# The second cross-attention layer's scores, softmax and attention rewritten in the form of the first layer's

## The chip, the cores and the metric

The kernel runs on one core of a Trainium2 chip. The time is device microseconds of one execution. The kernel before took 649.7 us, the median of three runs (649.56 to 650.06).

A core has TensorE (PE, matmuls; an fp32 matmul shows as two records in the profile), VectorE (DVE), ScalarE (ACT), GpSimd (POOL) and SyncE (SP, which here issues most of the loads). Each engine works through its own queue in order. Matmuls write to PSUM, in tiles of 128 × 512 fp32, of which the program has eight; everything else lies in SBUF.

## The reference

Two cross-attention layers over eight batches: 100 queries of 1024 features, 1444 context rows of 512 features. All is fp32.

```python
# layer 0
Q = query @ Wq + bq;  K = key @ Wk + bk;  V = key @ Wv + bv
weights = softmax(Q @ K.T / sqrt(1024), axis=-1)      # over the 1444 context rows
x = query + (weights @ V) @ Wo + bo
# layer 1
q = x @ Wq + bq;  k = latent @ Wk + bk;  v = latent @ Wv + bv
w = softmax(q @ k.T / sqrt(1024), axis=1)             # over the 100 queries
y = w @ v + x
out = (y - mean(y)) * rsqrt(var(y) + 1e-6) * gamma + beta
```

The axes of the two softmaxes differ: the first layer normalises over the context rows, the second over the queries of one batch. So in the second layer the weights of a context row sum to one, and those of a query don't: their sum, a column of 100 numbers per batch, multiplies `bv`.

## The kernel before

*Algebra.* The weight matrices are multiplied together first (Wq·Wk and, in layer 0, Wv·Wo), in the seven products of a Strassen-Winograd scheme (`weight_products`, `seven_products`). Then `queries(layer, …)` turns the queries into `gT[layer]`, 512 features by 400 queries per half of the batches, and scores are products of these with the raw context. Attention multiplies weights with the raw context, and the value projection comes after it (`project0`, and in layer 1 `project1_halves` for batches 0 to 4, `project1` for 5 and 6, `project_last` for 7). In these projections VectorE adds each product onto the residual `xT` (L585, L755), and some later products add onto the PSUM banks of earlier ones. Bias terms of the keys come in as one number per query (`c0`, `c1`).

*Layer 0.* The context comes in twice: as features (`load_features`, 128 features by 1444 rows, four loads `cT` per batch) and as rows (`load_rows`, chunks of 120 rows by 512 features, four units `c`). Scores (`scores0`, L528) have the queries loaded as weights and the features streamed, so they come out 100 queries by 1444 rows; in four PSUM banks. ACT copies them to `prob` with scale and bias (L541), VectorE takes maxima, ACT exponentials and normalises, and VectorE transposes the result in blocks of 32 × 32 to rows by queries (`transposed`, L563, 16 instructions of 12 blocks each per 32 partitions). Where that would be late, a few chunks are transposed by TensorE (`first_transposed`, L578). Attention (`weighted_rows`, L496) has the context rows loaded as weights and streams the 100 weights columns; it yields 512 features by 100 queries.

*Layer 1.* Scores (`scores1`, L643) have context columns loaded and stream the queries, so they come out 120 rows by 100 queries, and the softmax over queries is along the free axis. A PSUM bank holds a group of four chunks; for each of three groups VectorE scales and adds the bias (L653), takes maxima (L661), ACT does four exponentials with sums (L663), and VectorE reciprocal and product (L666, L667). Attention of batches 0 to 5 (`attend1`, L703) has the weights loaded and streams the context rows with a column of ones behind them (the memsets L470), so that the last column gives the sum of a query's weights; four TensorE transposes (`attended`, L723) turn it round. For batches 6 and 7 it is `weighted_rows`, and the sums come from VectorE (`weight_sums`, L679 to L681) and a transpose (`weight_totals`, L687).

*Order.* TensorE's order is written out by hand: the scores, attention and finishing routines are generators that yield after each matmul, and the loops at the end interleave them. A stage is the attention of batch b (48 matmuls) beside the scores of batch b+2 (44 steps in layer 0, 48 in layer 1). The first two batches' scores stand alone before the stages; in layer 0 the scores of the last batch run two steps to one. After stage 5 of layer 1 `project1_halves` runs with no attention beside it; batches 6 and 7 have `finish` routines (transposes L774, layer norm L778 to L797, output) beside their attention. The other engines' queues are put in order by a scheduler when the program is built.

*Memory.* One pool `stream` of ten equal units holds context loads and, earlier, weights. `weight_rows` has three buffers, `prob` three (in layer 1 these hold `bv`, `gamma` and `beta`, one number per feature, repeated on all partitions by `row_on_all`, L867). PSUM: six banks in `bank`, two in `bank2`.

## Time and profile before

| what | value |
|---|---|
| median of three runs | 649.7 us |
| the profiled execution | 649.66 us, of which 647.9 us from first to last instruction |
| granted TensorE clock, mean | 0.996 |
| bytes moved | 127.49 MB, 197 GB/s mean |
| layer 0: two batches' scores | 190.2 to 210.1 us |
| layer 0: stages and attention of the last batches | 210.1 to 350.3 us |
| projection and layer 1's queries | 350.3 to 426.2 us |
| layer 1: two batches' scores | 426.2 to 447.9 us |
| layer 1: six stages | 447.9 to 569.2 us |
| half-projection (`project1_halves`) | 569.2 to 593.0 us |
| last two batches, finishing | 593.0 to 647.9 us |

The profile page gives, for each engine, the busy time, its share of the span and the number of instructions; below it the span in 40 equal slices of 16.2 us with the busy tenths of each. A group line names the line of the program, the engine, the operation, output and inputs, and the shapes. The timeline gives the start, the length and the group; successive matmuls overlap a little, so the time of one is taken from start to start. In the second layer's stages the other engines' busy time is:

```profile
core 0: us, PE busy (x) PEld busy (x) DVE busy (x) ACT busy (x) POOL busy (x), PEclk, DMA share, GB/s
...
488.00:508.00 20.00, 20.00 (x196) 20.00 (x195) 5.69 (x12) 5.78 (x28) 0.41 (x4) 1.00 0.92 299
```

### The profile page before, as it was taken

To read this page: it belongs to the slowest core of one execution; us is meant where nothing else is said; L and a number is where in the kernel's file an instruction comes from. 1 tells how busy PE (TensorE), PEld (TensorE's weight loads), DVE (VectorE), ACT (ScalarE), POOL (GpSimd) and SP (SyncE) were. 2 spreads that over 40 slices of the span, in tenths; PEclk is the share of its full clock that TensorE was granted. 3 is DMA by queue.
4 is the path that set the end of the run, shared out by engine and by line. 5 is a ranking of instruction groups with operands and counts; after the bars stand their busy time and mean duration, and the time that the engine had idled before them with its cause. 6 is when DMAs were issued, how large, how long until landed. Compare 5 with 4: busy or idle time off the path is not lost.

```text
span 647.9 us, 10121 instructions
## 1 busy us (share of the span) xinstructions
PE 637.1 (98%) x4120; PEld 530.4 (82%) x4120; DVE 395.9 (61%) x751; ACT 122.6 (19%) x325; POOL 64.0 (10%) x81
## 2 busy tenths in 40 slices
PE   9999999999999999999999999999999999999994
PEld 7886445568885999999998555589999999989992
DVE  5999949569624775566753784266322223566984
ACT  1010010101104223322320001113222322210221
POOL 5000000019100000000000000000000000000673
PEclk9999999999999999999999999999999999999998
DMA  8928028000099888898998002038889999920212
GB/s 297 385 100 299 0 75 309 0 1 0 2 342 335 272 305 310 314 313 313 336 352 300 1 12 119 0 115 265 284 314 290 314 305 292 309 84 1 65 64 76
DMA packets 60234, 127.49 MB, mean 197 GB/s; under 512 B 3928, under 2 KB 22972, under 8 KB 60188
## 3 DMA queue, kind: packets, MB, share of 16 engines
q1 hardware_dynamic: 57742, 119.92, 54.2%
q0 software_dynamic: 2048, 6.56, 3.1%
q8 instruction: 32, 0.52, 0.3%
q10 hardware_dynamic: 398, 0.36, 0.2%
q14 instruction: 14, 0.11, 0.1%
HBM read 123.56 MB, written 3.28 MB: 196 GB/s over the span
## 4 chain that ended last, share of the span: by engine, by line
PE 81%; issue 11%; POOL 4%; DMA 1%; DVE 1%; POOLq 0%; ACT 0%; SPq 0%
PE A L496 12%; PE s L528 12%; PE s L643 10%; PE A L703 6%; PE qk_x L135 5%; PE g_x L135 5%; PE qk_y L135 4%; PE g_y L135 3%; PE vo_x L135 3%; PE o_x L135 3%; POOL z L796 3%; PE qk_w L135 2%; PE vo_y L135 2%; PE A1r L703 2%; PE o_y L135 2%
## 5 line engine op out<-in xcount | busy, mean ns | idle before, releaser
L496 PE MATMUL A<-w,c 120*128 120x100 f32 x960 | 145.0, 267 | 0.0
L496 PEld LDWEIGHTS A<-w,c 120*128 120x128 f32 x960 | 130.1, 191 | 0.3
L643 PE MATMUL s<-g1T,cT 128*120 128x100 f32 (+1 forms) x768 | 123.2, 261 | 0.0
L528 PE MATMUL s<-cT,g0T 128*100 128x131 f32 (+2 forms) x592 | 119.0, 296 | 0.0
L643 PEld LDWEIGHTS s<-g1T,cT 128*120 128x120 f32 (+1 forms) x768 | 105.2, 185 | 0.6 <-issue 0.3
L528 PEld LDWEIGHTS s<-cT,g0T 128*100 128x100 f32 x592 | 77.6, 167 | 8.3
L703 PE MATMUL A<-c,w 120*100 120x128 f32 (+1 forms) x432 | 83.0, 273 | 0.0
L563 DVE STREAM_TRANSPOSE w<-prob 32x384 f32<-32x384 f32 (+1 forms) x128 | 68.6, 536 | 15.3 <-ACT prob L549 12.5
L703 PEld LDWEIGHTS A<-c,w 120*100 120x100 f32 (+1 forms) x432 | 55.5, 168 | 0.0
L663 ACT ACTIVATE w<-w,negmax 120x100 f32<-120x100 f32 (+1 forms) x96 | 35.1, 366 | 76.7 <-DVE negmax L661 76.7
L653 DVE SCALAR_TENSOR_TENSOR w<-s,c 120x400 f32<-120x400 f32 (+1 forms) x24 | 13.8, 574 | 56.5 <-PE s L643 56.5
L541 ACT ACTIVATE prob<-s,c 100x394 f32<-100x394 f32 (+3 forms) x32 | 18.0, 563 | 94.5 <-PE s L528 94.3
L438 POOL TENSOR_SCALAR xT<-xT,L_xattn_bo 128x800 f32<-128x800 f32 x8 | 20.8, 2610 | 133.3 <-PE qk_x L135 133.3
L542 DVE TENSOR_REDUCE maxima<-prob 100x1 f32<-100x394 f32 (+3 forms) x32 | 16.3, 527 | 24.1 <-ACT prob L541 23.8
L135 PE MATMUL qk_x<-qk 128*128 128x256 f32 x128 | 29.1, 383 | 0.4 <-DMA qk<-in_L_xattn_WkT 0.4
L703 PE MATMUL A1r<-c,w 120*100 120x129 f32 x144 | 27.8, 274 | 0.0
L135 PEld LDWEIGHTS qk_x<-qk 128*128 128x128 f32 x128 | 23.8, 191 | 4.9 <-issue 1.4
L666 DVE RECIPROCAL rtotal<-total 120x4 f32<-120x4 f32 (+1 forms) x24 | 4.2, 176 | 28.9 <-ACT w L663 28.9
L277 DVE SCALAR_TENSOR_TENSOR qk_L_xattn_bk<-qk,L_xattn_bk,qk_L_xattn_bk 128x1024 f32<-128x1024 f32 x14 | 17.9, 1277 | 4.3 <-DMA qk<-in_L_xattn_WqT 4.2
L470 POOL MEMSET c<- 128x3 f32 x24 | 2.5, 104 | 162.7 <-PE s L643 140.0
L703 PEld LDWEIGHTS A1r<-c,w 120*100 120x100 f32 x144 | 18.5, 168 | 0.0
L585 DVE TENSOR_TENSOR xT<-xT,o_x 128x400 f32<-128x400 f32 (+1 forms) x24 | 13.7, 601 | 7.9 <-PE o_x L135 7.5
(230 smaller groups left out, 917.9 us busy)
## 6 DMA issues: line engine op xcount, KB each, us to landing
c<-in_ctx SPq DMA_DIRECT2D x48, 768.0 KB, 7.8
cT<-in_ctxT SPq DMA_DIRECT2D x32, 728.0 KB, 7.2
cT<-in_ctxT SPq DMA_DIRECT2D x32, 722.0 KB, 6.6
c<-in_ctx SPq DMA_DIRECT2D x16, 512.0 KB, 8.5
vo<-in_L_xattn_Wo SPq DMA_DIRECT2D x8, 512.0 KB, 6.4
qk<-in_L_xattn_WqT SPq DMA_DIRECT2D x8, 512.0 KB
qk<-in_L_xattn_WqT SPq DMA_DIRECT2D x15, 256.0 KB, 5.3
qk<-in_L_xattn_WkT SPq DMA_DIRECT2D x15, 256.0 KB, 6.7
```

Source lines behind the costliest of these rows:

```text
L135: nc.tensor.matmul(banks[n // per][:, n % per * width : (n % per + 1) * width], lhs[i][:, n * P : (n + 1) * P], rhs[i], start=(fresh and i ...
L277: nc.vector.scalar_tensor_tensor(acc, src, cols[v][:, h : h + 1], acc, ALU.mult, ALU.add)
L438: nc.gpsimd.tensor_scalar(xT[:, e, :], xT[:, e, :], out_bias[:, e : e + 1], None, ALU.add)
L496: nc.tensor.matmul(ps[:, k * T : (k + 1) * T], c[m // CQ][:r, m % CQ, k * P : (k + 1) * P], w[:r, m, :], start=(m == 0 and k == 0), stop=( ...
L528: nc.tensor.matmul(banks[n // per][:T, cuts[n] - o : cuts[n + 1] - o], q0[:, k, t0 : t0 + T], cT[k][:, cuts[n] : cuts[n + 1]], start=(k == ...
L541: nc.scalar.activation(p[:, o:e], ps[:T, : e - o], AF.Identity, bias=c0[:T, b : b + 1], scale=SCALE)
L542: nc.vector.tensor_reduce(parts[:, n : n + 1], p[:, o:e], AX.X, ALU.max)
L563: nc.vector.transpose(blocks(w, r, m0 * T + q * QD, T, MC - m0), blocks(p, q, m0 * MR + r * QD, MR, MC - m0),)
L643: nc.tensor.matmul(ps[:r, (m - m0) * T : (m - m0 + 1) * T], cT[m // CQ][:, k, o : o + r], q1[:, k, t0 : t0 + T], start=(k == 0), stop=(k = ...
L663: nc.scalar.activation(w[:r, m, :], w[:r, m, :], AF.Exp, bias=negmax[:r, m : m + 1], accum_out=total[:r, m : m + 1])
L703: nc.tensor.matmul(to, w[:r, m, :], c[m // CQ][:r, m % CQ, k * P : (L + 1 if k == LC - 1 else (k + 1) * P)], start=(m == 0 and k in (0, LC ...
L796: nc.gpsimd.tensor_tensor(z, z, beta[:T], ALU.add)
```

## The change

The second layer takes the first layer's routines, which become common ones (`scores`, `alternated`, `first_scores`).

- Scores: queries loaded as weights, features streamed (`load_features` in place of `load_columns`); ACT copies the raw scores, scaled and with the bias, to `prob`.
- Key bias: `key_biases`, as in layer 0, one column per batch, for both halves before the first scores; the matmuls against `ones` (L620) go.
- The raw scores are transposed by VectorE (`transposed`, 16 instructions) for batches 1 to 7; for batch 0 by TensorE, in three groups of four chunks placed between the scores of batch 1. Then the softmax by rows as before (`softmax_rows`), without the L653 step.
- Attention is `weighted_rows` for all batches; `attend1`, `attended` and the ones column go.
- The weights' sums: for every batch seven GpSimd instructions (`weight_sums`), and for each pair of batches two TensorE transposes and one VectorE reduction (`weight_totals`), at the ninth step of the odd batch's attention.
- The operand sums of the half-projection (`project1_sums`, eight instructions) move from VectorE to GpSimd.
- `gamma`, `beta` and the two halves of `bv` lie in two units of `stream`, for the whole of layer 1, and come in four GpSimd-issued loads; `prob` is used for scores.
- Layer 1's last scores run two steps to one, too.

Layer 0's work stays as it was.

```diff
     def unit(name):
-        return stream.tile([P, CQ * (L + 1)], F32, tag="unit", name=name)
+        return stream.tile([P, E + L], F32, tag="unit", name=name)
...
-    def left_sums(A, S, some=(0, 1, 2, 3)):
+    def left_sums(A, S, some=(0, 1, 2, 3), engine=nc.vector):
         A11, A12, A21, A22 = A
         todo = ((S[0], A21, A22, ALU.add), (S[1], S[0], A11, ALU.subtract))
         todo += ((S[2], A11, A21, ALU.subtract), (S[3], A12, S[1], ALU.subtract))
         for n in some:
-            combine(*todo[n])
+            combine(*todo[n], engine)
...
+    def key_biases(name, kb, bqbk):
+        sums = quarter_sums(name)[:, :B, :]
+        t = row(f"{name}_t").rearrange("p (b q j) -> p b q j", q=P // QD, j=QD)
+        for g in range(B // G):
+            src = bass.AP(kb[g].tensor, kb[g].offset, [list(kb[g].ap[0]), [T, G], [QD, P // QD], [1, QD]])
+            nc.vector.transpose(t[:, g * G : (g + 1) * G], src)
+        nc.vector.tensor_reduce(sums, t, AX.X, ALU.add)
+        c = totals(name, sums, B)
+        nc.vector.tensor_scalar(c, c, SCALE, bqbk, ALU.mult, ALU.add)
+        return c
...
-    def load_columns(b):
...
-    def load_rows(b, summed=False):
+    def load_rows(b):
         src = a["ctx_512"][b]
         for q in range(NQ):
             t = unit(f"c_{b}_{q}").rearrange("p (c l) -> p c l", c=CQ)
-            if summed:
-                nc.gpsimd.memset(t[:, :, L:], 1.0)
-            t = t if summed else t[:, :, :L]
             n = CQ - (q == NQ - 1)
...
-                    nc.sync.dma_start(out=t[r0:r1, n, :L], in_=src[m + r0 : m + r1, :])
+                    nc.sync.dma_start(out=t[r0:r1, n, :], in_=src[m + r0 : m + r1, :])
             yield t
...
-    def scores0(s, cT, alone=False):
+    def scores(s, layer, cT, softmax, alone=False):
         b = s["b"]
-        p = prob[b % len(prob)][:T, :S]
-        q0 = gT[0][b // G]
+        p = s["p"] = prob[b % len(prob)][:T, :S]
+        q = gT[layer][b // G]
         t0 = b % G * T
...
-        parts = small.tile([T, NB], F32, tag="maxima", name=f"maxima_{b}")
-        for n, ps in enumerate(banks):
-            o, e = cuts[n * per], cuts[min((n + 1) * per, n_pieces)]
-            nc.scalar.activation(p[:, o:e], ps[:T, : e - o], AF.Identity, bias=c0[:T, b : b + 1], scale=SCALE)
-            nc.vector.tensor_reduce(parts[:, n : n + 1], p[:, o:e], AX.X, ALU.max)
+        parts = [slice(cuts[n * per], cuts[min((n + 1) * per, n_pieces)]) for n in range(NB)]
+        for part, ps in zip(parts, banks):
+            nc.scalar.activation(
+                p[:, part],
+                ps[:T, : part.stop - part.start],
+                AF.Identity,
+                bias=key_bias[layer][:T, b : b + 1],
+                scale=SCALE,
+            )
+        w = s["rows"] = weight_rows(f"w{layer}_{b}")
+        s["w"] = w[:, : MC * T].rearrange("p (c t) -> p c t", t=T)
+        softmax(s, parts)
+        yield
...
-    def first_transposed(s):
-        b, p = s["b"], prob[s["b"] % len(prob)][:T]
-        ps = bank(f"pT_{b}")
+    def first_transposed(s, m0):
+        b, p, r = s["b"], s["p"], shown(m0)
+        ps = bank(f"pT_{b}_{m0}")
         for m in range(PT):
-            nc.tensor.transpose(ps[:MR, m * T : (m + 1) * T], p[:, m * MR : (m + 1) * MR], ident[:T, :T])
-        nc.scalar.copy(s["rows"][:MR, : PT * T], ps[:MR, : PT * T])
+            o = (m0 + m) * MR
+            nc.tensor.transpose(ps[:r, m * T : (m + 1) * T], p[:, o : o + r], ident[:T, :T])
+        nc.scalar.copy(s["rows"][:r, m0 * T : (m0 + PT) * T], ps[:r, : PT * T])
...
-    def key_bias1(g):
...
-    def scores1(s, cT, c1):
...
+    def softmax1(s, parts):
+        if s["b"]:
+            transposed(s, 0)
+            for m in range(0, MC, GM):
+                softmax_rows(s, m)
+            weight_sums(s)
+    def softmax_rows(s, m0):
+        b, w, r = s["b"], s["w"], shown(m0)
+        grp = slice(m0, m0 + GM)
+        negmax, total, rtotal = (
+            small.tile([P, GM], F32, tag=n, name=f"{n}_{b}_{m0}") for n in ("negmax1", "total1", "rtotal1")
+        )
+        nc.vector.tensor_reduce(negmax[:r], w[:r, grp, :], AX.X, ALU.max, negate=True)
+        for m in range(GM):
+            nc.scalar.activation(
+                w[:r, m0 + m, :], w[:r, m0 + m, :], AF.Exp, bias=negmax[:r, m : m + 1], accum_out=total[:r, m : m + 1]
             )
...
+        nc.vector.reciprocal(rtotal[:r], total[:r])
+        nc.vector.tensor_tensor(
+            w[:r, grp, :], w[:r, grp, :], rtotal[:r].unsqueeze(2).to_broadcast([r, GM, T]), ALU.mult
+        )
     def weight_sums(s):
         b, w = s["b"], s["w"]
-        part = work.tile([P, T], F32, tag="part", name=f"part_{b}", bufs=1)
-        wsum = s["wsum"] = work.tile([P, T], F32, tag="wsum", name=f"wsum_{b}", bufs=2)
+        part = work.tile([P, L], F32, tag="half", name=f"part_{b}", bufs=1)[:MR, : 5 * T]
+        part = part.rearrange("p (c t) -> p c t", t=T)
+        wsum = s["wsum"] = work.tile([P, T], F32, tag="wsum", name=f"wsum_{b}", bufs=3)
         last = MC - 1
         n = held(last)
-        nc.vector.tensor_copy(wsum[:n], w[:n, last, :])
-        nc.vector.tensor_reduce(part[:MR], w[:MR, :last, :].rearrange("p c t -> p t c"), AX.X, ALU.add)
-        nc.vector.tensor_tensor(wsum[:MR], wsum[:MR], part[:MR], ALU.add)
-    def weight_totals(s):
...
-    def attend1(s, c):
...
-    def attended(s, dst):
...
+        add = nc.gpsimd.tensor_tensor
+        add(part, w[:MR, 0:5, :], w[:MR, 5:10, :], ALU.add)
+        add(part[:, 0:2, :], part[:, 0:2, :], part[:, 2:4, :], ALU.add)
+        for more in (part[:, 1, :], part[:, 4, :], w[:MR, 10, :]):
+            add(part[:, 0, :], part[:, 0, :], more, ALU.add)
+        nc.gpsimd.tensor_copy(wsum[:n], w[:n, last, :])
+        add(wsum[:MR], wsum[:MR], part[:, 0, :], ALU.add)
+    def weight_totals(pair):
+        n = held(MC - 1)
+        ps = bank(f"wsum_ps_{pair[0]['b']}")[:T, : 2 * n].rearrange("p (b n) -> p b n", n=n)
+        for i, s in enumerate(pair):
+            nc.tensor.transpose(ps[:, i, :], s["wsum"][:n, :], ident[:n, :n])
+        r = small.tile([T, 2], F32, tag="r", name=f"r_{pair[0]['b']}", bufs=B // 2)
+        nc.vector.tensor_reduce(r, ps, AX.X, ALU.add)
+        for i, s in enumerate(pair):
+            s["r"] = r[:, i : i + 1]
...
     def project1_sums(w):
         t = weights.tile([P, LC, E], F32, tag="w", name="wv1_s")
         A = [[w[:, 2 * k + i, h * 512 : h * 512 + 512] for i in range(2)] for h in range(2) for k in range(2)]
         S = [[t[:, n, i * 512 : i * 512 + 512] for i in range(2)] for n in range(4)]
-        left_sums(A, S)
+        left_sums(A, S, engine=nc.gpsimd)
         return A, S
...
-    run(scores0(batches[0], *loaded(load_features(0)), alone=True))
-    s0 = scores0(batches[1], *loaded(load_features(1)), alone=True)
-    for n in range(LC * NB):
-        next(s0)
-        if n == LC * NB - 3:
-            first_transposed(batches[0])
-    for b in range(B):
+    def first_scores(layer, softmax, between):
+        for b in range(2):
+            steps = scores(batches[b], layer, *loaded(load_features(b)), softmax, alone=True)
+            for n in range(LC * NB):
+                next(steps)
+                if b == 1 and n in between:
+                    between[n]()
+    def alternated(b, layer, softmax, dst, doubled=False):
         nxt = b + 2 < B
         c, *cT = loaded(load_rows(b), *([load_features(b + 2)] if nxt else []))
-        A = weighted_rows(batches[b]["w"], c, A0[b // G][:, :, b % G * T : (b % G + 1) * T], f"A0_{b}")
-        s0 = scores0(batches[b + 2], *cT) if nxt else iter(())
-        for n in range(MC * LC):
+        A = weighted_rows(batches[b]["w"], c, dst, f"A{layer}_{b}")
+        ahead = scores(batches[b + 2], layer, *cT, softmax) if nxt else iter(())
+        for _ in range(MC * LC):
             next(A)
-            for _ in range(2 if b + 3 == B else 1):
-                next(s0, None)
+            for _ in range(2 if doubled else 1):
+                next(ahead, None)
+            yield
+    key_bias = [c0, None]
+    first_scores(0, softmax0, {LC * NB - 3: lambda: first_transposed(batches[0], 0)})
+    for b in range(B):
+        steps = alternated(b, 0, softmax0, A0[b // G][:, :, b % G * T : (b % G + 1) * T], b + 3 == B)
+        for n, _ in enumerate(steps):
             if (b, n) == (B - 2, MC * LC - PT - 1):
-                first_transposed(batches[B - 1])
+                first_transposed(batches[B - 1], 0)
         if b == 1:
             AS = value_sums(wvo)
     project0(AS, A0)
-    def row_on_all(name, n):
-        t = prob[n][:, :E]
-        nc.gpsimd.dma_start(out=t, in_=a[name].partition_broadcast(P))
-        return t
     gT[1] = queries(1, wqk1, u1)
-    c1 = [key_bias1(0)]
-    bv1 = row_on_all("L1_xattn_bv", 0)
-    gamma = row_on_all("L1_xattn_gamma", 1)
-    beta = row_on_all("L1_xattn_beta", 2)
+    kb1 = [key_bias_sums(f"kb1_{g}", g * GT, (g + 1) * GT, wqbk1) for g in range(B // G)]
+    key_bias[1] = key_biases("c1", kb1, bqbk1)
+    vectors = [unit(f"vectors_{j}") for j in range(2)]
+    gamma, beta = (t[:, :E] for t in vectors)
+    bv1 = [t[:, E:] for t in vectors]
+    for name, t in (("gamma", gamma), ("beta", beta)):
+        nc.gpsimd.dma_start(out=t, in_=a[f"L1_xattn_{name}"].partition_broadcast(P))
+    for j, t in enumerate(bv1):
+        nc.gpsimd.dma_start(out=t, in_=a["L1_xattn_bv"][j * 512 : (j + 1) * 512].partition_broadcast(P))
     wv1 = weights.tile([P, LC, E], F32, tag="w", name="wv1")
     nc.gpsimd.dma_start(out=wv1, in_=a["L1_xattn_Wv"].rearrange("(c p) e -> p c e", p=P))
-    for b in range(2):
-        run(scores1(batches[b], *loaded(load_columns(b)), c1[0]))
-    c1.append(key_bias1(1))
+    def first_rows(m0):
+        first_transposed(batches[0], m0)
+        softmax_rows(batches[0], m0)
+        if m0 == MC - GM:
+            weight_sums(batches[0])
+    first_scores(1, softmax1, {5 + m0 // 2: lambda m0=m0: first_rows(m0) for m0 in range(0, MC, GM)})
     A1 = {}
     finished = {(B - 2, 0): 0, (B - 2, 14): 1, (B - 2, 28): 2, (B - 1, 6): G1, (B - 1, 22): G1 + 1}
     finishing = []
     for b in range(B):
-        nxt = b + 2 < B
         if b in (0, G1, B - 1):
             n = {0: G1, G1: 2, B - 1: 1}[b]
             t = work.tile([P, LC * G1 * T], F32, tag="AT", name=f"A1T_{b}", bufs=2)
             t = t[:, : LC * n * T].rearrange("p (c t) -> p c t", c=LC)
             for i in range(n):
                 A1[b + i] = (t, t[:, :, i * T : (i + 1) * T])
-        c, *cT = loaded(load_rows(b, nxt), *([load_columns(b + 2)] if nxt else []))
-        if nxt:
-            A = attend1(batches[b], c)
-            s1 = scores1(batches[b + 2], *cT, c1[(b + 2) // G])
-        else:
-            A = weighted_rows(batches[b]["w"], c, A1[b][1], f"A1_{b}")
-            s1 = iter(())
-        for n in range(MC * LC):
-            next(s1, None)
-            next(A)
-            if n == 10 and 1 <= b <= B - 2:
-                attended(batches[b - 1], A1[b - 1][1])
+        for n, _ in enumerate(alternated(b, 1, softmax1, A1[b][1], b + 3 == B)):
+            if b % 2 and n == 8:
+                weight_totals(batches[b - 1 : b + 1])
             if (b, n) in finished:
                 finishing.append(finish(batches[finished[b, n]]))
             finishing = [f for f in finishing if next(f, finishing) is not finishing]
-        if not nxt:
-            weight_totals(batches[b])
         if b == B - 1:
             run(untransposed(batches[b]))
-        if B - 3 <= b < B - 1:
-            weight_sums(batches[b + 1])
         if b == 1:
             AS = project1_sums(wv1)
         if b == G1:
```

## The prediction

> **What bounds the kernel now.** First the busy shares and the clock on the page.
>
> ```profile
> PE 637.1 (98%) x4120; PEld 530.4 (82%) x4120; DVE 395.9 (61%) x751; ACT 122.6 (19%) x325; POOL 64.0 (10%) x81
> ...
> PE   9999999999999999999999999999999999999994
> ...
> DVE  5999949569624775566753784266322223566984
> ...
> PEclk9999999999999999999999999999999999999998
> ```
>
> TensorE (PE) never rests and its clock is granted in full: the time is the length of its queue, and anything else counts only where PE waits. So I read PE in order of time, where both layers' forms of one job stand side by side (start, length, then the group).
>
> ```profile
> 190.24 18.45 PE L528 MATMUL s<-cT,g0T 128*100 128x361 f32 x60
> 208.53 0.51 PE L578 MATMUL pT<-ident,prob 100*120 100x100 f32 x4
> ...
> 228.83 1.25 PE L496 MATMUL A<-w,c 124*128 124x100 f32 x10
> ...
> 307.33 1.25 PE L496 MATMUL A<-w,c 124*128 124x100 f32 x10
> ...
> 322.55 15.77 PE L496 MATMUL A<-w,c 120*128 120x100 f32 x140
> ...
> 426.17 0.83 PE L620 MATMUL c_ps<-kb,ones 128*128 128x400 f32 x2
> 426.84 20.52 PE L643 MATMUL s<-g1T,cT 128*120 128x100 f32 x192
> ...
> 447.89 0.35 PE L643 MATMUL s<-g1T,cT 128*120 128x100 f32 x2
> ...
> 569.19 3.54 PE L135 MATMUL o_x<-A1T,wv 128*128 128x250 f32 x16
> ```
>
> The L496 lines stand four stages apart: a first-layer stage (attention of one batch beside scores of the batch two ahead) takes (307.33 − 228.83)/4 = 19.62 us. A second-layer stage, 447.89 to 569.19 over six, takes 20.22, in which a transpose L723 is included (472.35 to 492.63, two of them, is 20.28). One fp32 matmul is two records.
>
> **PE's own sum.** *First scores*: now 426.17 to 447.89, 21.72 us. Then: a small sum for the key bias (L323 costs 0.2), 32 matmuls at the price of L528's 60 records (18.29 us to the next line: 0.61 per matmul, 19.51) and 12 transposes like L578 (four take 0.35: 1.05). 20.76; saves 0.96. *Six stages*: now 121.30. Then five of 19.62; the sixth with doubled score steps as in the first layer (22 steps at 0.65, from L528 lines at 309.08, 309.73, 310.38, then 26 attention matmuls at 2 × 15.60/140 = 0.223: 20.1); and three pairs of transposes for the weights' sums (L687 to the next line is 0.10 each, 0.6). 118.8; saves 2.5. *Tail*: the L723 transpose in batch 6 goes (596.13 to 596.48, 0.35); the last pair of L687 was there before. Sum: −3.8 us. All else on PE stands unchanged. It goes wholly to the end only if PE still never waits, so each wait is costed next.
>
> **Work moved to VectorE, ScalarE (ACT) and GpSimd (POOL).** Per batch the scores now leave PSUM by four ACT copies (0.53 to 0.59 each, L541) in place of three L653; VectorE (DVE) gains 16 transposes L563, which take 9.46 from 217.81 to 227.27; the softmax by rows keeps its instructions: L661 0.5 from start to start, four exponentials of one group 1.55 (455.76 to 457.32), L666 0.17, L667 0.5. In a steady stage starting at t, scores of the batch ahead end one us early, transposes run t−0.1 to t+9.3, the three groups are ready at t+13, t+14 and t+15.5. They are wanted at t+19.6: 6 us of cover on DVE, which idles there (5.69 busy of 20). Cost nothing. With the first two batches there is no such stage. Batch 0's first group: its transposes stand after six matmuls of batch 1's scores (439.8), copy 0.5, maximum 0.5, exponentials 1.55, reciprocal and product 0.8: 443.8, wanted at 447. Batch 1: ACT takes its scores up to 449.7, transposes to 459.2, all groups to 465.2, wanted at 466.6. Cover 1.4 at worst; nothing, and whatever exceeds it is paid.
>
> The Trainium skill (VectorE: DVE Perf Modes, Rules for kernel authors) speaks against this part: a full 128 × 128 transpose belongs on TensorE, block transposes on VectorE. Its way would, by L578, cost PE 1.05 us for each of seven batches, 7.4 in sum, so it would turn the gain into a loss of 3.6; by the L563 row the nine us lie under cover except in one place, the next.
>
> **The wait I expect: the half-projection after stage 5** (569.19 to 593.0, seven products of 3.4 us). There DVE must fold each product into the residual, because later products add onto the same banks. In DVE's queue of the changed kernel the last batch's 16 transposes stand before the first of these folds, and its softmax between them. With t the start of stage 5: batch 6's softmax ends at t+15.5 and its exponentials hold ACT till 14.75; ACT's four copies of batch 7's scores end at t+16.9; transposes end at t+26.4. Stage 5 ends at t+20.3 (20.1 and 0.2), so that is 6.1 after its end. From there to the end of the first fold of the fourth product the queue holds: seven folds L585 (0.58 each, last one 0.65), three maxima, three reciprocals, three products, four operand sums L146 (0.34 each): 4.1 + 1.5 + 0.5 + 1.5 + 1.4 = 9.0, ending 15.1 after the stage. Its readers wait: the fifth product adds onto that bank and would start at 13.5 (579.32 to 582.7 is the fourth now, 569.19 the stage's end). PE loses 1.6. Bounds: none, if the chain is 1.6 shorter; 3.0, if GpSimd's sums of batch 7, which then run, hold up an operand sum with two SBUF inputs, as L793 is held up beside L796 (1274 ns least, 2683 most: 1.4 more). I take 1.6, as most ops in the chain have one SBUF input.
>
> **Weights' sums on GpSimd.** 500 + 200 + 5 × 100 columns. No such row; lower bound by L796's 2356 ns for 1024 columns: 1200 × 2.3 = 2.8 us; upper bound by L801 (256 columns, 1013 ns) as the price of each small one and 1.44 for the big one on the line between the two rows: 7.5. I take 4.8: 2.8 and seven gaps of 0.28, the gap between L796 and L797. PE wants batch 1's sum at 466.6 + 9 × 0.427 = 470.4; ready 465.2 + 4.8 = 470.0. Cost 0, bounds 0 and 2.3. PE's in-order queue would stand behind this transpose, scores and attention both. Later pairs are wanted 8 us after their rows are ready (t+15.5 against t+23.5), the third 10.7 after: nothing. The ones column's 24 memsets L470 on GpSimd and the key-bias matmuls go; that cost no path. By the skill (GPSIMD Engine Reference, Elementwise side-by-side) an add there takes 1.96 times VectorE's; on the 2.6 us of L679 to L681 that would make 5.1, ready at 470.3: still no wait.
>
> **The rest at nothing.** Key bias of batches 4 to 7 earlier: one scaled product, seven L356 (0.63), two block transposes L433 (0.68) and a reduction (1.2) move into 370 to 398 on DVE, about 7.4 us; DVE's waits for PE in there are 1.5, 1.4, 0.2, 0.4, 0.7, 0.3 and 4.2, 8.7 in sum. If that cover failed, the folds before the queries' second product (393.8) would be late by the excess, at most 1. Weight differences for the half-projection: eight of 512 columns on GpSimd, 9.4 by L796's rate, 426 to 436, needed after 560. SP issues as many loads as before; POOL four for the three vectors instead of three, before the large load that waits for PE till 386. The vectors take two of ten stream buffers.
>
> Sum, against the execution's own 649.66 (span 647.9 and 1.8 around it; the median shown is 649.7, so they can be read as one): 649.7 − 3.8 + 1.6 = **647.5 us**.
>
> **Rivals.** *No wait at all* (the chain after stage 5 shorter): 645.9. For it: the DVE rows are maxima of dense stretches; against: two sets of 9.46 in one stage. *The wait eats the gain*: it needs 3.8, so DVE 2.2 us later than I count; 649.7. For it: ACT and DVE hand over a dozen times in that chain. *Slower, the sums starve*: if GpSimd's adds can't run beside DVE's transposes, batch 1's sum, begun at 465.2, stops at 466.7 and resumes at 476.2, ready at 479.5: PE waits 9 us, 656.5; it decides from a sum that takes over 5.2 us. Against: L433's two transposes ran beside L438 in 661 and 697 ns, L317's of that size alone in 699 to 703. *Slower, the loads come late*: with eight buffers a unit is asked for three quarters of a stage, 14.7 us, ahead instead of 24.5 − 4.9 = 19.6. Each us to landing above 14.7 costs a us in five stages; at 16 the sum is 647.5 + 6.5 = 654. Against:
>
> ```profile
> c<-in_ctx SPq DMA_DIRECT2D x48, 768.0 KB, 7.8
> cT<-in_ctxT SPq DMA_DIRECT2D x32, 728.0 KB, 7.2
> cT<-in_ctxT SPq DMA_DIRECT2D x32, 722.0 KB, 6.6
> ```
>
> The loads land in half of that, and the first layer's form (722 KB) soonest. *It doesn't do what it says*: excluded for PE, whose new queue repeats the first layer's stages.
>
> **How the numbers follow.** A measurement of this kernel tells 0.2%, 1.3 us, from no change: faster is below 648.4. Forecast 0.52, with its own range 646.0 to 649.0 (the wait's bounds are 0 and 3.0); no wait 0.10; eaten gain 0.17; starving sums 0.11; late loads 0.10. Of the forecast 0.06 lies above 648.4. Faster 0.52 − 0.06 + 0.10 = 0.56, same 0.17 + 0.06 = 0.23, slower 0.21. The range goes from no wait, rounded down, into the slower cases: 645.5 to 653.0; what lies above is most of the starving and part of the late loads, some 0.15, below 0.03.
>
> **What would show it.** Stages of 19.62 in the second layer and no PE wait there show the sum right. A gap of PE between the fourth and the fifth product of the half-projection, ended by a DVE fold, shows the wait, its length the size. A PE gap at the first sums' transposes (470) with POOL behind it, or at a stage's start with DMA behind it, would make the forecast wrong, as would DVE transposes longer than 0.59.

## The result, and the profile after

The changed kernel takes 647.4 us, the median of seven runs (646.99 to 647.88), beside 649.7 us for seven of the kernel before on the same chip (649.56 to 650.52). The ratio is 0.9962, with a 95% interval of 0.9951 to 0.9974: faster, by a little. The profiled execution of the changed kernel took 647.25 us, 645.5 from first to last instruction, against 649.66 and 647.9 before.

From the changed kernel's page: the busy sums and, of the 40 slices, VectorE's row and the clock's. TensorE is as full as before with 184 fewer instructions, VectorE is busier by 43 us (395.9 to 438.8), GpSimd by 38 (64.0 to 102.4), and the clock is still granted in full.

```profile
PE 634.1 (98%) x3936; PEld 519.3 (80%) x3936; DVE 438.8 (68%) x831; ACT 134.6 (21%) x342; POOL 102.4 (16%) x122
...
DVE  5999959569624775566753887214767655896994
...
PEclk9999999999999999999999999999999999999998
```

TensorE in order of time (start, length, group; in brackets the idle time ahead and what ended it). The second layer begins at 425.82, its stages at 446.52; the half-projection begins at 565.41 and the next attention at 590.58.

```profile
425.82 0.30 PE L323 MATMUL c<-c_sums,same 128*128 128x32 f32 x2
425.96 13.60 PE L515 MATMUL s<-cT,g1T 128*100 128x361 f32 x44
439.40 0.51 PE L578 MATMUL pT<-ident,prob 100*120 100x100 f32 x4
...
446.52 0.36 PE L486 MATMUL A<-w,c 120*128 120x100 f32 x2
...
469.98 0.38 PE L661 MATMUL wsum_ps<-ident,wsum 124*100 124x124 f32 x2
...
485.10 1.25 PE L486 MATMUL A<-w,c 124*128 124x100 f32 x10
...
504.73 1.25 PE L486 MATMUL A<-w,c 124*128 124x100 f32 x10
...
565.41 3.56 PE L135 MATMUL o_x<-A1T,wv 128*128 128x250 f32 x16
...
575.56 3.54 PE L135 MATMUL o_x<-A1T,wv_s 128*128 128x250 f32 x16
580.35 3.64 PE L135 MATMUL o_x<-A1T,wv_s 128*128 128x250 f32 x16 [1.26 <-DVE xT L585]
...
590.58 0.36 PE L486 MATMUL A<-w,c 120*128 120x100 f32 x2
```

From such lines each kernel's time falls into stretches. The second layer begins at 425.5 to 427.1 in the runs below. That spread arises in the first 20 us, as the opening weight loads land sooner or later (TensorE waits up to 1.4 us for one of them): from the weight product that begins at 20.00 in the kernel before and at 19.66 in the changed one, both take 406.2 us to the second layer, and so do all the others. So the last column, counted from there to the end, compares best.

| kernel | median us | first scores | six stages | half-projection | rest | layer 1 to end |
|---|---|---|---|---|---|---|
| before | 649.7 | 21.72 | 121.30 | 23.81 | 54.9 | 221.7 |
| changed | 647.4 | 20.70 | 118.89 | 25.17 | 54.9 | 219.7 |
| e1_products_pool | 646.95 | 20.70 | 118.89 | 24.25 | 54.9 | 218.7 |
| e2_first_chunks_pe | 646.57 | 20.70 | 119.23 | 23.84 | 54.9 | 218.7 |
| e10_products_and_sums_pool | 646.58 | 20.70 | 118.89 | 23.89 | 54.9 | 218.3 |
| e3_sums_vector | 653.83 | 20.71 | 118.88 | 31.36 | 54.9 | 225.9 |
| e4_all_transposes_pe | 654.62 | 20.70 | 125.52 | 23.83 | 55.7 | 225.7 |
| e5_four_vector_units | 647.82 | 20.71 | 120.24 | 23.83 | 54.9 | 219.7 |
| e8_sums_twice | 650.99 | 20.71 | 122.85 | 25.17 | 55.0 | 223.7 |
| e11_sums_longer | 649.41 | 20.71 | 120.73 | 25.15 | 54.9 | 221.4 |
| e9_operand_sums_vector | 647.42 | 20.70 | 118.89 | 25.17 | 54.9 | 219.6 |
| e6_attention_alone | 654.33 | 21.72 | 125.97 | 23.88 | 54.7 | 226.3 |
| e7_scores_alone | 669.59 | 20.70 | 139.83 | 26.43 | 54.9 | 241.9 |

The kernel before took 649.9 to 650.1 us beside the experiments. The gain: 1.02 in the first scores and 2.41 in the stages, of which 1.36 is given back in the half-projection. In the kernel before, TensorE did not wait there; its fourth and fifth product stand in one line without a gap:

```profile
579.32 7.10 PE L135 MATMUL o_x<-A1T,wv_s 128*128 128x250 f32 x32
...
593.00 0.36 PE L496 MATMUL A<-w,c 120*128 120x100 f32 x2
```

VectorE of the changed kernel at that place. The transposes of the last batch end 5.9 us after the stage, and from there the queue is dense; the fold that the fifth product waits for is the first of the pair at 579.63, done at 580.3.

```profile
561.81 9.46 DVE L562 STREAM_TRANSPOSE w<-prob 32x384 f32<-32x384 f32 x16 [1.07 <-ACT prob L527]
571.30 0.68 DVE L585 TENSOR_TENSOR xT<-xT,o_x 128x500 f32<-128x500 f32 x1
...
577.93 1.25 DVE L585 TENSOR_TENSOR xT<-xT,o_y 128x500 f32<-128x500 f32 x2
579.10 0.61 DVE L146 TENSOR_TENSOR A1T<-A1T 128x250 f32<-128x250 f32 x1
579.63 1.25 DVE L585 TENSOR_TENSOR xT<-xT,o_x 128x500 f32<-128x500 f32 x2
```

GpSimd's sums for batch 1: begun at 464.37, done at 468.30, 3.94 us, and 1.7 ahead of TensorE's transposes at 469.98 above.

```profile
464.37 1.26 POOL L649 TENSOR_TENSOR part<-w 120x500 f32<-120x500 f32 x1 [12.52 <-ACT prob L527]
...
467.90 0.40 POOL L654 TENSOR_TENSOR wsum<-wsum,part 120x100 f32<-120x100 f32 x1
```

### The profile page after: what moved, and what is told of

The parts are those of the page before. It is cut to its first block, busy times and chain, and to the rows that moved or that the text cites. A ratio compares the mean times of both kernels' runs of the same rounds, so it can differ in the third digit from the quotient of the medians.

```text
span 645.5 us, 9860 instructions
## 1 busy us (share of the span) xinstructions
PE 634.1 (98%) x3936; PEld 519.3 (80%) x3936; DVE 438.8 (68%) x831; ACT 134.6 (21%) x342; POOL 102.4 (16%) x122
## 4 chain that ended last, share of the span: by engine, by line
PE 84%; issue 5%; POOL 5%; DVE 3%; ACT 2%; POOLq 0%; ACTq 0%; DVEq 0%
PE s L515 23%; PE A L486 20%; PE qk_x L135 7%; PE g_x L135 5%; PE qk_y L135 4%; PE g_y L135 3%; PE vo_x L135 3%; DVE w L562 3%; PE o_x L135 3%; POOL z L737 2%; PE qk_w L135 2%; PE qk_z L135 2%; PE vo_y L135 2%; PE o_y L135 2%; PE g_w L135 2%
## 5 line engine op out<-in xcount | busy, mean ns | idle before, releaser
L486 PE MATMUL A<-w,c 120*128 120x100 f32 (+1 forms) x1536 | 242.8, 266 | 0.0
L486 PEld LDWEIGHTS A<-w,c 120*128 120x128 f32 (+1 forms) x1536 | 213.6, 190 | 0.5
L562 DVE STREAM_TRANSPOSE w<-prob 32x384 f32<-32x384 f32 (+1 forms) x240 | 132.4, 552 | 38.1 <-POOL wsum L654 16.6
L515 PE MATMUL s<-cT,g1T 128*100 128x131 f32 (+2 forms) x592 | 119.4, 296 | 0.0
L515 PE MATMUL s<-cT,g0T 128*100 128x131 f32 (+2 forms) x592 | 119.0, 296 | 0.0
L515 PEld LDWEIGHTS s<-cT,g0T 128*100 128x100 f32 x592 | 77.6, 167 | 8.3
L515 PEld LDWEIGHTS s<-cT,g1T 128*100 128x100 f32 x592 | 77.5, 167 | 7.7
L527 ACT ACTIVATE prob<-s,c 100x393 f32<-100x393 f32 (+2 forms) x64 | 35.1, 559 | 123.3 <-PE s L515 122.9
L649 POOL TENSOR_TENSOR part<-w 120x500 f32<-120x500 f32 x8 | 10.0, 1246 | 114.8 <-PE s L515 47.3
L630 DVE TENSOR_REDUCE negmax<-w 120x4 f32<-120x400 f32 (+1 forms) x24 | 12.7, 555 | 13.2 <-ACT w L579 13.1
L632 ACT ACTIVATION_READ_ACCUMULATOR w<-w,negmax 120x1 f32 (+1 forms) x96 | 17.9, 186 | 0.0
L737 POOL TENSOR_TENSOR z<-z,vectors 100x1024 f32<-100x1024 f32 x7 | 16.5, 2356 | 8.3 <-ACT z L736 8.3
```

Of the source, the lines that this page charges most:

```text
L486: nc.tensor.matmul(ps[:, k * T : (k + 1) * T], c[m // CQ][:r, m % CQ, k * P : (k + 1) * P], w[:r, m, :], start=(m == 0 and k == 0), stop=( ...
L515: nc.tensor.matmul(banks[n // per][:T, cuts[n] - o : cuts[n + 1] - o], q[:, k, t0 : t0 + T], cT[k][:, cuts[n] : cuts[n + 1]], start=(k == ...
L527: nc.scalar.activation(p[:, part], ps[:T, : part.stop - part.start], AF.Identity, bias=key_bias[layer][:T, b : b + 1], scale=SCALE,)
L562: nc.vector.transpose(blocks(w, r, m0 * T + q * QD, T, MC - m0), blocks(p, q, m0 * MR + r * QD, MR, MC - m0),)
L630: nc.vector.tensor_reduce(negmax[:r], w[:r, grp, :], AX.X, ALU.max, negate=True)
L632: nc.scalar.activation(w[:r, m0 + m, :], w[:r, m0 + m, :], AF.Exp, bias=negmax[:r, m : m + 1], accum_out=total[:r, m : m + 1])
```

## The experiments

**What makes the wait of 1.26 us?** First, the last batch's products leave VectorE's queue:

```diff
-        nc.vector.tensor_tensor(
+        engine = nc.gpsimd if b == B - 1 else nc.vector
+        engine.tensor_tensor(
             w[:r, grp, :], w[:r, grp, :], rtotal[:r].unsqueeze(2).to_broadcast([r, GM, T]), ALU.mult
```

> The changed kernel, with the last batch's three normalising products (0.57 us each on VectorE) on GpSimd, so that VectorE's queue between the last batch's transposes and the fold of the fourth product is 1.7 us shorter. Theory (VectorE's queue makes TensorE's 1.26 us wait at the fifth product of the half-projection): that wait falls to 0 to 0.2 us, the half-projection goes from 25.2 to 23.8 or 24.0, the time from 647.4 to 646.1. Rival (the wait comes from the late transposes or from ScalarE's twelve exponentials, which end at 576.8): the wait stays, 647.4. Second rival (GpSimd's products beside VectorE's folds stretch both): a wait of 0.5 to 1.3 us stays, 646.6 to 647.4.

Measured: a wait of 0.34, the half-projection at 24.25. VectorE's queue is the cause, since 0.92 of the wait went with the three products; ScalarE and the transposes were unchanged. The expectation allowed 0.2 at most. What it missed is the second rival's kind of loss, at another place: the two operand sums, 0.74 us a pair beside nothing, took 1.37 here, while GpSimd worked at a product (576.97 to 577.91). The timelines of VectorE, TensorE and GpSimd in this run, one fence each:

```profile
574.27 0.74 DVE L146 TENSOR_TENSOR A1T<-A1T,o_t 128x250 f32<-128x250 f32 x2
...
576.80 1.37 DVE L146 TENSOR_TENSOR A1T<-A1T 128x250 f32<-128x250 f32 x2
```

```profile
580.28 3.64 PE L135 MATMUL o_x<-A1T,wv_s 128*128 128x250 f32 x16 [0.34 <-DVE xT L585]
```

```profile
576.97 0.94 POOL L637 TENSOR_TENSOR w<-w,rtotal 120x400 f32<-120x400 f32 x1 [0.79 <-DVE rtotal L635]
```

Second, from the other side, a shorter transpose on VectorE for 0.35 us of TensorE:

```diff
+            first = PT if s["b"] == B - 1 else 0
-            transposed(s, 0)
-            for m in range(0, MC, GM):
+            transposed(s, first)
+            for m in range(first, MC, GM):
...
+            if (b, n) == (G1, MC * LC - PT - 1):
+                first_transposed(batches[B - 1], 0)
+                softmax_rows(batches[B - 1], 0)
+                weight_sums(batches[B - 1])
```

> The changed kernel, with the first four chunks of the last batch's scores transposed by TensorE near the end of stage 5, as batch 0 has it; VectorE's sixteen transposes take 0.44 us instead of 0.57 (7.0 instead of 9.46 together, by the first layer's rows of the same kernel). Theory (the queue's length makes the wait): TensorE pays 0.35 us more, VectorE's queue ends 2.4 us sooner, so the 1.26 us wait goes: 647.4 + 0.35 - 1.3 = 646.4. Rival (the wait hangs on something else in that stretch): 647.7.

Measured: no wait, the half-projection at 23.84, the stages 0.34 longer, as expected. Third, products and two operand sums together on GpSimd, so that the two no longer meet:

```diff
-        seven_products("o1", A, Bs, S, T_, 4, n, add, add, right=lambda k: right_sums(Bs, T_, (k,)))
+        seven_products("o1", A, Bs, S, T_, 4, n, add, add, right=lambda k: right_sums(Bs, T_, (k,), nc.gpsimd if k == 3 else nc.vector))
```

> The changed kernel, with the last batch's three normalising products and the last two operand sums of the half-projection (L146, for the sixth product) on GpSimd. In the run with the products alone the wait was 0.34 us, and those two operand sums took 1.37 us in place of 0.72 beside a GpSimd product. Theory (what was left is that collision): VectorE's queue is 1.4 us shorter again, the fifth product does not wait, the half-projection takes 23.8, the time is 0.3 us under the run with the products alone, 0.9 to 1.4 under the changed kernel: 646.0. Rival (ScalarE's exponentials hold the third reciprocal, and the folds stand behind it): 0.2 to 0.4 of wait stays. Rival (the operand sums come late on GpSimd): a wait at the sixth product instead, 646.5 to 647.5.

Measured: no wait is listed for this product any more, the half-projection takes 23.89, which is 1.28 shorter than in the changed kernel, and layer 1 to the end is 1.3 shorter. But the fold came only 0.36 sooner after the stage's end than in the first of these runs, not 1.4, because VectorE now stands 1.07 us for a GpSimd product. By its stretches this is the shortest version of the study. By its runs the ratio to the kernel before is 0.9947 (0.9934 to 0.9959); that interval overlaps the changed kernel's, so the better version is told by the stretches, not by the medians.

**Is it right to keep the sums off VectorE?**

```diff
-        add = nc.gpsimd.tensor_tensor
...
-        add(wsum[:MR], wsum[:MR], part[:, 0, :], ALU.add)
+        nc.vector.tensor_copy(wsum[:n], w[:n, last, :])
+        nc.vector.tensor_reduce(part[:MR], w[:MR, :last, :].rearrange("p c t -> p t c"), AX.X, ALU.add)
+        nc.vector.tensor_tensor(wsum[:MR], wsum[:MR], part[:MR], ALU.add)
```

> The changed kernel, with the weights' sums of all batches back on VectorE (2.6 us a batch: copy 0.2, reduction 2.15, add 0.25). Theory (VectorE has about 4 us to spare in a stage, and none in the half-projection): stages 1 to 4 unchanged at 19.6; batch 6's sums end at 563.3 instead of 560.7, so the last transposes start 1.5 us later, and batch 7's sums stand before the fold of the fourth product, 2.6 more: the wait at the fifth product goes from 1.26 to 5.4, the time from 647.4 to 651.5. Rival (the sums' engine does not matter, only the softmax): 647.4. Rival on the other side (GpSimd's sums hold up VectorE in every stage, so that taking them away speeds it up): below 647.

Measured: stages 118.88, unchanged, and a wait of 4.92 instead of the 5.4 expected; but the half-projection grew by 6.2, not by 4.1. The rest stands in the product behind the wait, 6.17 us in TensorE's timeline for what takes 3.6, and in the windows of the same run: there a line has the stretch, its length, the busy time and instructions of PE, PEld, DVE, ACT and POOL, then the granted clock, the DMA share and the GB/s.

```profile
583.73 6.17 PE L135 MATMUL o_x<-A1T,wv_s 128*128 128x250 f32 x16 [4.92 <-DVE xT L585]
```

```profile
580.00:582.00 2.00, 0.00 (x0) 0.00 (x0) 2.00 (x2) 0.00 (x0) 0.00 (x0) 1.00 0.00 0
582.00:584.00 2.00, 0.27 (x1) 0.30 (x2) 2.00 (x5) 0.00 (x0) 0.00 (x0) 0.52 0.00 0
584.00:586.00 2.00, 2.00 (x6) 1.60 (x6) 0.17 (x1) 0.00 (x0) 0.00 (x0) 0.50 0.00 0
```

**How near was the starved-sums rival?** The sums done twice over, first wholly, then all but the last add:

```diff
+        for _ in range(2):
             add(part, w[:MR, 0:5, :], w[:MR, 5:10, :], ALU.add)
...
             add(wsum[:MR], wsum[:MR], part[:, 0, :], ALU.add)
```

> The changed kernel, in which GpSimd works out the weights' sums of every batch twice, with the same result: 3.9 us more of GpSimd in each stage. Theory (GpSimd's sums run beside VectorE undisturbed and are covered, with 1.7 us to spare at batch 1 and 4 or more elsewhere): batch 1's sum is ready at 472.3 instead of 468.3 and TensorE, which wants it at 470.0, waits 2.3 us there; nowhere else: 649.7. Rival (GpSimd is starved beside VectorE's dense stretches): batch 1's second round takes twice its time or more, a wait of 6 us or more, 653 and above. Rival (the first stage has no such edge): 647.4.

Measured: a wait of 2.12 us at the place foreseen and no other new one; GpSimd's second round took the same 3.9 us beside VectorE's transposes, so nothing starves. But the stages grew by 3.96. Behind the wait the clock fell again (timeline of TensorE, then the windows):

```profile
472.08 0.39 PE L662 MATMUL wsum_ps<-ident,wsum 124*100 124x124 f32 x1 [2.12 <-POOL wsum L655]
472.26 0.60 PE L486 MATMUL A<-w,c 120*128 120x100 f32 x2
472.65 0.65 PE L515 MATMUL s<-cT,g1T 128*100 128x131 f32 x2
```

```profile
472.00:474.00 2.00, 1.92 (x10) 1.93 (x11) 1.89 (x5) 0.00 (x0) 0.02 (x1) 0.55 0.17 60
474.00:476.00 2.00, 2.00 (x13) 2.00 (x13) 1.94 (x5) 0.00 (x0) 0.00 (x0) 0.60 0.24 28
476.00:478.00 2.00, 2.00 (x21) 2.00 (x20) 0.79 (x4) 1.85 (x11) 0.00 (x0) 1.00 0.88 338
```

A matmul of 0.36 us takes 0.60, and so for some 3.4 us. Eight of ten executions took 650.9 to 651.4 us at a mean clock of 0.992 or 0.993; two took 649.4 and 649.7 at 0.995 and 0.996, about the price of the bare wait. So the same wait costs its length once or nearly twice. (That the clock stayed up in those two is read from their mean; only one execution of a run has a timeline.)

> The changed kernel, in which GpSimd works out all but the last add of the weights' sums twice, with the same result: 3.55 us more a batch instead of 4.0. TensorE waits 1.66 us at batch 1's sum, instead of 2.12. In the run with 4.0 more the granted clock fell to 0.55 to 0.6 for some 3.5 us behind that wait, which made the six stages 1.85 longer than the wait alone, in eight of ten executions; behind the changed kernel's wait of 1.26 it stayed at 1.00. Theory (the clock falls in any execution in which the gap meets some window, so a shorter gap meets it more seldom): some executions near 649.1 and some near 650.8, with fewer of the latter than eight in ten. Rival (a fixed limit between 1.66 and 2.12): all near 649.1. Rival (a fixed limit between 1.26 and 1.66): all near 650.8.

Measured: a wait of 1.64 us, and the clock stays at 1.00 behind it (again TensorE's timeline and the windows):

```profile
473.13 0.31 PE L662 MATMUL wsum_ps<-ident,wsum 124*100 124x124 f32 x1 [1.64 <-POOL wsum L655]
```

```profile
472.00:474.00 2.00, 0.87 (x8) 0.87 (x9) 1.96 (x4) 0.00 (x0) 0.92 (x3) 1.00 0.56 231
474.00:476.00 2.00, 2.00 (x21) 2.00 (x20) 1.91 (x4) 0.00 (x0) 0.00 (x0) 1.00 0.39 36
```

All eleven executions (648.8 to 650.4) have a mean clock of 0.995 to 0.997, none the lower one. So at this place a gap of 1.64 us did not bring the drop, and one of 2.12 did in eight of ten executions. Length alone does not decide: in the run with the scores alone (below) TensorE waited 2.35 us in the half-projection, and the clock stayed at 1.00 behind it.

```profile
596.15 2.80 PE L135 MATMUL o_y<-o_t,wv_s 128*128 128x250 f32 x12 [2.35 <-DVE xT L588]
```

That speaks against a fixed limit and fits the first theory, a window that the gap has to meet; no run here varied the moment of a gap by itself, so the window is not shown. The Trainium skill (TensorE: Matmul & The Clock Gate, Why this matters for your kernels) asks for no gaps over some 3 us; here 2.12 was already too long in most executions.

**Whose place are the transposes?** All on TensorE:

```diff
-            transposed(s, 0)
...
+            if b + 1 < B and n in (8, 16, 24):
+                first_rows((n - 8) // 2, b + 1)
```

> The changed kernel, with the raw scores of all batches transposed by TensorE, twelve a batch, three groups of four in the stage ahead of the batch's own, and none by VectorE. Theory (TensorE is the bound in every stage, VectorE's transposes lie under cover save in the half-projection): seven batches at 1.05 us (four transposes take 0.35) make 7.35 more on TensorE, the 1.35 us of the half-projection's wait go: 647.4 + 7.35 - 1.35 = 653.4, with stages of 20.7 instead of 19.6. Rival (VectorE's transposes hold the stages back, and TensorE's own take less beside other work): 647 or less.

Measured: 654.6 us; stages longer by 6.63 (18 groups at 0.37), the rest by 0.8 (the last three), the wait gone. From layer 1 to the end that is 6.0 more, as expected, if 0.02 more a group: TensorE bounds every stage. The other 1.2 between the two medians lies outside that stretch: in the profiled execution the second layer begins 0.45 later, and 0.9 more stands outside the span from first to last instruction. The rule of the Trainium skill weighed in the prediction (VectorE: DVE Perf Modes, Rules for kernel authors) would have turned the gain of 2.3 into a loss of 4.7.

**Loads and operand sums.** Four stream buffers for the vectors, so six for the loads:

```diff
-    vectors = [unit(f"vectors_{j}") for j in range(2)]
+    vectors = [unit(f"vectors_{j}") for j in range(4)]
...
```

> The changed kernel, with the three vectors spread over four stream buffers instead of two, so that six are left for the loads and a load is asked for 9.8 us ahead (half a stage) instead of 14.7. Theory (loads land 6.6 to 8.5 us after they are asked for, the lead is ample): 647.4, at most 0.5 more. Rival (the transfers are near their limit, since the DMA share is 0.9 in the stages): TensorE waits for DMA at the quarters of each stage; a landing of 11 us would cost 1.2 us in each of five stages, 653.

Measured: the first waits for loads, 0.86 us in two, both in stage 5, whose scores run two steps to one; the stages grew by 1.35 in all, and the half-projection lost its wait, because VectorE's transposes had that time to get ahead (they end 4.5 us after the stage instead of 5.9). The end is where it was: 219.7. Executions scatter more (647.1 to 651.7, the longest at a mean clock of 0.990). With six buffers waits for loads show, with eight none. TensorE's timeline of the run with six:

```profile
553.50 0.69 PE L515 MATMUL s<-cT,g1T 128*100 128x131 f32 x4 [0.28 <-DMA cT<-in_ctxT]
557.81 0.47 PE L515 MATMUL s<-cT,g1T 128*100 128x131 f32 x2 [0.58 <-DMA cT<-in_ctxT]
```

The half-projection's operand sums back on VectorE:

```diff
-        left_sums(A, S, engine=nc.gpsimd)
+        left_sums(A, S)
```

> The changed kernel, with the half-projection's eight operand sums of 512 columns back on VectorE, as before. Theory (they cost nothing on either engine, needed 130 us later than they are made): 647.4, the same stages. Rival (on VectorE they delay batch 0's first weights, wanted at the start of the first stage): a wait there, 648 or more.

Measured: 647.4, all stretches the same. That part of the change is worth nothing here.

**Which half of the change gains in the stages?** Two kernels that each take one half, attention or scores, and leave the other in the old form:

```diff
-        if nxt:
-            A = attend1(batches[b], c)
-            s1 = scores1(batches[b + 2], *cT, c1[(b + 2) // G])
-        else:
-            A = weighted_rows(batches[b]["w"], c, A1[b][1], f"A1_{b}")
-            s1 = iter(())
+        A = weighted_rows(batches[b]["w"], c, A1[b][1], f"A1_{b}")
+        s1 = scores1(batches[b + 2], *cT, c1[(b + 2) // G]) if nxt else iter(())
...
```

> The kernel before, with only the second layer's attention in the first layer's form (weighted rows, no transposes of its result, weights' sums by VectorE for all batches); its scores keep the kernel before's form. TensorE's rows: a score matmul of the old form takes 0.195 us from start to start beside another form, an attention matmul of the new form 0.20 beside another form (L496 before L774) and 0.223 alone. Theory (the six stages' gain is the attention's, and the scores' new form costs 0.7 us a stage): 48 steps of 0.395 and the sums' transposes, 19.0 to 19.1 a stage, 114.4 for six instead of 121.3, no wait in the half-projection: 649.7 - 6.9 = 642.8. Rival (the attention's new form takes 0.223 here too): 48 steps of 0.418, 120.9 for six, 649.3. Rival (the gain is the scores'): 649.7 or more.

```diff
-        A = weighted_rows(batches[b]["w"], c, dst, f"A{layer}_{b}")
+        A = attend1(batches[b], c) if summed else weighted_rows(batches[b]["w"], c, dst, f"A{layer}_{b}")
...
```

> The changed kernel, with the second layer's attention of batches 0 to 5 in the kernel before's form (ones column, result transposed by TensorE, no weights' sums but for batches 6 and 7); its scores keep the changed kernel's form. Theory (new scores cost more than old ones in a stage: 44 at 0.228 against 48 at 0.195): 48 attention matmuls at 0.22, 44 scores at 0.228 and 0.35 of transposes, 20.9 a stage, about 125.3 for six instead of 118.9; the half-projection keeps its wait of 1.3: 647.4 + 6.4 = 653.8. Rival (the gain of the stages is the scores': 44 at 0.202): 19.8 a stage, 118.9 for six, 647.4.

Measured: the attention alone makes the kernel slower than before, 654.3 us, with six stages of 126.0. The theory and the first rival were wrong; the second rival's number, 649.7 or more, held, but not its reason, since the scores alone lose too. They take 20.9 a stage, as expected, against 20.2 before (the transposes L703 at 471.65 and 492.53 stand 20.88 apart). The whole, 669.6 us, is no measure of them: TensorE waits 12.5 us in stage 5 for ScalarE's copies of the attention's result, which wait for GpSimd's sums of batch 6, whose partial sums use the same buffer. That wait is the edit's own, and the clock was at 0.50 behind it for some 4.6 us. The half-projection's wait is another one as well: 2.35 at the third product, not 1.3 at the fifth. TensorE's timeline at the same place of four kernels, one fence each: before, attention alone, scores alone, changed.

```profile
452.03 0.35 PE L643 MATMUL s<-g1T,cT 128*120 128x100 f32 x2
452.22 0.38 PE L703 MATMUL A<-c,w 120*100 120x128 f32 x2
452.44 0.35 PE L643 MATMUL s<-g1T,cT 128*120 128x100 f32 x2
```

```profile
452.01 0.37 PE L643 MATMUL s<-g1T,cT 128*120 128x100 f32 x2
452.22 0.39 PE L496 MATMUL A<-w,c 120*128 120x100 f32 x2
452.45 0.37 PE L643 MATMUL s<-g1T,cT 128*120 128x100 f32 x2
```

```profile
452.02 0.38 PE L683 MATMUL A<-c,w 120*100 120x128 f32 x2
452.24 0.39 PE L518 MATMUL s<-cT,g1T 128*100 128x131 f32 x2
452.46 0.38 PE L683 MATMUL A<-c,w 120*100 120x128 f32 x2
```

```profile
452.06 0.36 PE L486 MATMUL A<-w,c 120*128 120x100 f32 x2
452.25 0.39 PE L515 MATMUL s<-cT,g1T 128*100 128x131 f32 x2
452.48 0.36 PE L486 MATMUL A<-w,c 120*128 120x100 f32 x2
```

In the shapes, "120*128" is the loaded matrix (128 columns), "120x100" the streamed one (100 columns). A step is the time from one start to the next. It is short, 0.19 to 0.20, when it streams 100 columns and the next one loads 100: L643 before L703, L486 before L515. If the next loads 120 or 128, the same L643 takes 0.21 to 0.22, and the attention's 100 columns (L496) 0.22 to 0.23; a step that streams 128 or more takes 0.22 to 0.23, whatever comes next. So a pair is cheap when a narrow stream is followed by a narrow load: 0.414 on average before and 0.425 after. With either half changed alone no narrow stream meets a narrow load, and a pair costs 0.43 to 0.45. What the whole change gains in the stages is then count, since its pair is a little dearer: 44 pairs at 0.425 and four attention matmuls alone at 0.223 make 19.6, where 48 pairs at 0.414 and 0.35 for the transposes of the attention's result made 20.2.

## Why the prediction was right

- *First scores*, 20.76 foreseen: 20.70. *Six stages*, 118.8: 118.89. The rows of the first layer's stages held because the pair was taken whole; the split by matmul, tried later in the attention's run, failed by 11.6 us in 114.4.
- *Tail*, 0.35: nearly nothing, 54.9 us before and after. The transpose went, but most of its time came back: 0.18 of it at the projection of batches 5 and 6, which begins 1.06 after the transposes ahead of it (603.38 to 604.44) instead of 0.88; the rest in smaller amounts that were not followed. The prediction put nothing against this term, and it is the one that failed.
- *The wait*, 1.6 at the fifth product by VectorE's fold: 1.26, and 1.36 in the stretch. Its chain: transposes foreseen to end 6.1 after the stage, measured 5.9; from there 9.0 foreseen, 9.0 measured (571.27 to 580.28). So the mechanism is the one foreseen. The upper bound's mechanism, an operand sum held up beside GpSimd, is real but small here (0.61 for 0.39), and 0.6 us in the run with the products on GpSimd.
- *Sums on GpSimd*, 4.8 (2.8 to 7.5): 3.94, no wait. The add of 500 columns took 1.25, those of 100 columns 0.39 to 0.43. On VectorE the same sums take 2.6 (the run with the sums there), so GpSimd needs 1.5 times as long, less than the 1.96 that the prediction weighed.
- *Nothing* for key bias, operand sums and vectors: the 406.2 us ahead of the second layer and the stretches in it show none, and the operand sums were tried by themselves. (The copies L541 are read as 0.53 to 0.59; the shortest take 0.48. It moves nothing.)
- *Rivals.* No wait: the wait is there. Wait eats the gain: VectorE would have to be later, as in the run with the sums on it. Starving: shown wrong by the sums done twice. Late loads: they need two buffers fewer, and then lengthen the stages by 1.35 us.
- One step was wrong without harm: the rivals price a wait by its length. The 2.12 us wait cost 4.0 in most executions and the 4.92 us wait 7.5, so the starving rival's nine would probably have cost more than nine, and the eaten gain would have turned into a loss sooner.

647.5 was foreseen, 647.4 came, and that it is so near is in part luck. The tail saved some 0.3 less than foreseen and the stages 0.09 less; the wait cost 0.24 less and the first scores 0.06 less. So the second layer saved 2.05 instead of 2.2, and the profiled execution's second layer began 0.35 earlier than that of the kernel before, which is no work of the change.

## What to carry to other kernels

Where TensorE is full, price a change by whole repeating patterns that already stand in the trace; the price of a matmul depends on what the next one loads, so two halves that each lose can gain together. Then look for the one place where another engine's new work stands in its queue ahead of something TensorE needs: there, moving a microsecond of side work to an idle engine brings back what the change lost. And don't price a wait of TensorE by its length alone: here waits up to 1.64 us cost their length, and one of 2.12 mostly nearly twice that.

## What the runs showed of the hardware that was not expected

- TensorE's granted clock fell to about half with a gap of 2.12 us (for some 3.4 us; eight of ten executions, by their mean clock) and with one of 4.92 us (for some 6.8 us, from 582.1 to 588.9, and so from before the gap's end; all four executions). With gaps of 1.26 and 1.64 us it fell in no execution (seven and eleven, with means of 0.995 to 0.997), and with one of 2.35 us it did not fall in the one execution that has a timeline.
- The time from one fp32 matmul's start to the next depends on what the next one loads: the same L643, streaming 100 columns, took 0.19 to 0.20 us before a load of 100 columns and 0.21 to 0.22 before one of 128.
- A pair of VectorE adds of two SBUF inputs took 1.85 times as long beside a GpSimd product of two SBUF inputs (1.37 us for 0.74), while VectorE's transposes took their 9.46 us beside GpSimd's adds.
